# A macaron layer with float32 products from two float32r parts: filling PSUM banks in turns

## The chip, the cores and the metric

The kernel runs on one core of one Trainium2 chip. The metric is the device time of one launch in microseconds (us); every array is laid out by the host beforehand. The profile names the engines of the core as PE (TensorE matmul), PEld (its weight load), DVE (VectorE), ACT (ScalarE), POOL (GpSimd) and SP (SyncE, which issues DMAs here).

## The reference

The input x has the shape (4, 1024, 256) in float32. Three residual steps follow each other:

```python
x = x + 0.5 * ffn(layernorm(x), w1, w2, h1, h2, w3, scales)
x = x + attn(layernorm(x), log_dt, log_A_real, A_imag, C, W, b)
x = x + 0.5 * ffn(layernorm(x), w1, w2, h1, h2, w3, scales)

def tlin(x, w, s): return einsum('bsi,oi->bso', x, w) * s     # w holds only -1, 0 and 1
def ffn(x):                                                   # 256 -> 1024 -> 1024 -> 1024 -> 256
    h = silu(tlin(x, w1, w1_s)) * tlin(x, w2, w2_s)
    h = gelu(tlin(h, h1, h1_s))
    h = gelu(tlin(h, h2, h2_s))
    return tlin(h, w3, w3_s)
def attn(x):                                                  # S4D: a long convolution for each channel
    K = 2 * einsum('dn,dnl->dl', C', exp(dtA * t)).real       # taps of 1024 positions, 32 modes
    y = irfft(rfft(x_t, 2048) * rfft(K, 2048))[:, :, :1024]
    return gelu(y) @ W.T + b
```

## The kernel before

**Blocks and layers.** Each FFN works on 8 blocks of 512 tokens, named f0 to f7 in the first FFN and g0 to g7 in the second. f0 to f7, g0 and g1 go one by one through `ffn`; the last six go in three pairs through `ffn_pair`, whose wide layers are done with fewer products of half-size matrices. A wide input `t` is kept as two float32r parts: the high part is a cast on ACT (line 401), the low part is what the cast left, formed on DVE (`low_part`, line 309). Each linear layer then is two products for each 128 channels of input, one for each part, all summed in one PSUM bank (`linear`, lines 362 to 372, with the matmul at line 366). A bank of 128x512 float32 takes 4 products in the first layer (`pa` and `pb`, from `xt`), and 16 in the second and third (`p2`, `p3`, from `ha` and `h2`). The output layer takes 16 products for each of two banks (`po`, from `h3`, line 617 in `last_squares`). Behind each bank ACT applies silu or gelu (lines 384 and 399), and the next layer reads the result.

**Side work.** All else goes in between as a second stream. `kernel_steps` forms the S4D taps: sines and exponentials on ACT, products on DVE (`a_b`, `k_b`, `qd`, `p`), small matmuls into `pk` (line 883). `kernel_spectrum` takes their spectrum (`pf`). `mix` does the convolution of one batch and the multiplication by W (`pi`, line 1134, and `pw`, line 1159). The generator yields after a few operations, or yields PAUSE where it would wait. `tick` (line 1245) is called after each bank of a wide layer and lets side work run up to a count of work (STEP_WORK), or up to a PAUSE. `prepare` (line 1189), advanced by `ahead`, loads, normalises (`x_f`), moves and splits (`xt`) the next block. `weight_checks` (line 678) compares the weights with their signs on the fly, and sums the misses by one matmul (`p_bad`, line 724); if there were misses, a second copy of the layers would run.

**Order.** A scheduler reorders instructions within each engine when the program is built, by priorities and its own durations; then every engine runs its list in order and waits on semaphores. PSUM has 8 banks, all in one pool (tag "ps"). The names in the profile leave out the buffer numbers: `p_f` is p2 or p3 of some f block, `h_f` is h2 or h3.

Of the kernel before, what the change touches and what calls it, by code (L numbers as in the profile page):

```python
# [18 lines left out]
P = 128  # L19
B, L, D = 4, 1024, 256  # L20
HID = 1024
J = L // P
# [86 lines left out]
def macaron_layers(  # L109
# [24 lines left out]
    nc = tc.nc  # L134
# [224 lines left out]
            xt.append(t)  # L359
        return xt  # L360

    def linear(ps, w, m, acts):
        n = len(acts)
        for k in range(n):
            for part in range(parts):
                nc.tensor.matmul(  # L366
                    ps,
                    w[:, k, m * P : (m + 1) * P],
                    acts[k][:, part, :],
                    start=(k == 0 and part == 0),  # L370
                    stop=(k == n - 1 and part == parts - 1),
                )

    def ffn(xt, src, dst, blk, name, tick, ahead, final):


        ha = []
        for m in range(KH):
            pa, pb = bank(f"pa_{name}_{m}"), bank(f"pb_{name}_{m}")
            linear(pa, w1_sb, m, xt)  # L380
            linear(pb, w2_sb, m, xt)
            g = half(f"g_{name}_{m}")
            t = ring(f"ha_{name}_{m}", parts, TB, dtype=wide)
            nc.scalar.activation(g, pa, AF.Silu, scale=sc_sb[:, 0, m : m + 1])  # L384
            nc.vector.scalar_tensor_tensor(  # L385
                g if split else t[:, 0, :], pb, sc_sb[:, 1, m : m + 1], g, ALU.mult, ALU.mult
            )
            if split:
                nc.scalar.copy(t[:, 0, :], g)
                low_part(t, g)  # L390
            ha.append(t)
        for layer, w in ((2, h1_sb), (3, h2_sb)):
            hb = []
            for m in range(KH):
                ps = bank(f"p{layer}_{name}_{m}")
                linear(ps, w, m, ha)
                t = ring(f"h{layer}_{name}_{m}", parts, TB, dtype=wide)
                g = half(f"g{layer}_{name}_{m}") if split else t[:, 0, :]
                nc.scalar.activation(g, ps, AF.Gelu, scale=sc_sb[:, layer, m : m + 1])  # L399
                if split:  # L400
                    nc.scalar.copy(t[:, 0, :], g)  # L401
                    low_part(t, g)
                hb.append(t)
                ahead()
                if layer == 2 or m < KH - 1:
                    tick()
            ha = hb
        ahead(last=True)
        if name == "f0":
            nc.scalar.mul(w3s_half, w3s_half, 0.5)  # L410
        if final:
            last_tokens(ha, src, dst, blk, name)
        else:
            last_squares(ha, src, dst, blk, name)()

    def ffn_pair(xts, src, dst, blks, names, tick, ahead, final):

        pair_name = names[0]
        raw = raw_tiles(f"g_{pair_name}")
        for n, (xt, name) in enumerate(zip(xts, names)):  # L420
            for m in range(KH):
                pa, pb = bank(f"pa_{name}_{m}"), bank(f"pb_{name}_{m}")
                linear(pa, w1_sb, m, xt)
                linear(pb, w2_sb, m, xt)
                g = raw[m // QK, n][m % QK]
                nc.scalar.activation(g, pa, AF.Silu, scale=sc_sb[:, 0, m : m + 1])
                nc.vector.scalar_tensor_tensor(
                    g, pb, sc_sb[:, 1, m : m + 1], g, ALU.mult, ALU.mult
                )
            if n == 0:  # L430
                b11 = operand(raw[0, 0], f"b112_{pair_name}")
        calls = 0

        def step():
            nonlocal calls
            calls += 1
            if calls % 2 == 0:
                ahead()
                if calls < 2 * 7 * QK:
                    tick()  # L440

        raw, b11, _ = winograd(raw, b11, 2, pair_name, step)
        raw, c22, c12 = winograd(raw, b11, 3, pair_name, step)
        c11 = operand(raw[0, 0], f"hl00_{pair_name}")
        end_1 = last_squares(c12 + c22, src, dst, blks[1], names[1], QK)
        c21 = operand(raw[1, 0], f"hl10_{pair_name}")
        ahead(last=True)
        if final:
            end_1(nc.vector, nc.sync)
            last_tokens(c11 + c21, src, dst, blks[0], names[0])  # L450
        else:
            end_0 = last_squares(c11 + c21, src, dst, blks[0], names[0])
            end_1()
            end_0()
# [148 lines left out]
    def last_squares(acts, src, dst, blk, name, first=0):  # L603


        rest = []
        for k in range(DC):
            xr = half(f"xr_{name}_{k}", TB // SQ, SQ)
            for c in range(P // SQ):
                nc.sync.dma_start(xr[c * SQ : (c + 1) * SQ], in_squares(src, blk, k, c))  # L610
            rest.append(xr)
        banks = [bank(f"po_{name}_{k}") for k in range(DC)]
        order = [(first + k) % KH for k in range(KH)]
        for o, ps in enumerate(banks):
            for k in order:
                for part in range(parts):
                    nc.tensor.matmul(  # L617
                        ps,
                        w3_sb[:, k, o * P : (o + 1) * P],
                        acts[k][:, part, :],  # L620
                        start=(k == order[0] and part == 0),
                        stop=(k == order[-1] and part == parts - 1),
                    )

        def end(add_on=nc.gpsimd, queue=stores):
            for k, ps in enumerate(banks):
                o, y = half(f"o_{name}_{k}"), half(f"y_{name}_{k}", TB // SQ, SQ)
                nc.scalar.activation(o, ps, AF.Identity, scale=w3s_half[:, k : k + 1])
                nc.vector.transpose(y, o.rearrange("p (n s) -> p n s", s=SQ))  # L629
                add_on.tensor_tensor(y, rest[k], y, ALU.add)  # L630
                for c in range(P // SQ):
                    queue.dma_start(in_squares(dst, blk, k, c), y[c * SQ : (c + 1) * SQ])

        return end
# [198 lines left out]
    def kernel_steps():  # L833
# [7 lines left out]
        for g0 in range(0, DD, group):  # L841
# [58 lines left out]
            for d1 in range(0, group, n):  # L900
                re, im = fine

                def outer(coarse, t):
                    return (
                        coarse[:, d1 : d1 + n, :, None].to_broadcast(shape),
                        t[:, d1 : d1 + n, None, :].to_broadcast(shape),
                    )

                a, o = (half(f"{t}_{g0 + d1}", n, A1, A0) for t in ("p", "po"))
                tt(a, *outer(to_re, re), ALU.mult)  # L910
                tt(o, *outer(to_im, im), ALU.mult)
                tt(a, a, o, ALU.add)
                ready.append((d1, a))
                if len(ready) == 4:
                    for old in ready[0:2]:
                        products(*old)
                    del ready[0:2]
                yield
            yield PAUSE
            for old in ready:  # L920
# [115 lines left out]
    def mix(b, xn):  # L1036
# [109 lines left out]
        for j in range(0, J, 2):  # L1146
            xr = half(f"xr_{b}_{j}", 2, D)
            nc.sync.dma_start(xr, positions(x1, b, j))
            todo.append((j, xr))
            if len(todo) == 1:  # L1150
                continue
            yield PAUSE
            results = []
            for j, xr in todo:
                ps = bank(f"pw_{b}_{j}")
                results.append(ps)
                for e in range(2):
                    for dc in range(DC):
                        nc.tensor.matmul(  # L1159
                            ps[:, e * D : (e + 1) * D],  # L1160
                            yts[dc][j // JQ][:, (j % JQ + e) * P : (j % JQ + e + 1) * P],
                            wt_sb[:, dc, :],
                            start=(dc == 0),
                            stop=(dc == DC - 1),
                        )
            yield PAUSE
            for (j, xr), ps in zip(todo, results):
                y = half(f"yw_{b}_{j}", 2, D)
                tt(
                    y,  # L1170
                    ps.rearrange("p (e d) -> p e d", e=2),
                    bias_sb[:, None, :].to_broadcast([P, 2, D]),
                    ALU.add,
                )
                nc.gpsimd.tensor_tensor(y, xr, y, ALU.add)
                stores.dma_start(positions(x2, b, j), y)
            todo = []
# [208 lines left out]
```

## Time and profile before

| | us |
|---|---|
| median of 3 runs | 1369.99 |
| lowest and highest run | 1369.08, 1370.74 |
| the profiled execution | 1368.44 |
| its span | 1366.6 |
| PE busy in it | 1351.7 |
| DVE busy | 1010.7 |
| ACT busy | 776.5 |
| POOL busy | 287.9 |

The profile shows one execution. A row of its timeline has the start in us from the span's start, the busy time, the engine, the line, the operation, what it writes and reads, and how many instructions are merged into the row; in square brackets stands the idle time before the row and which engine's work ended it. The durations of rows overlap within an engine, since the next instruction starts before the last one's end is recorded: for what an instruction costs its engine, the distance between starts is used. PEclk is the granted clock of TensorE, in this execution 0.998 of full speed in the mean.

### The profile page before, as it was taken

Reading aid. Unit: us, or ns where it says so; the run is one execution under the profiler, and the core shown is the slowest. Engines: PE = TensorE matmul, PEld = TensorE weight load, DVE = VectorE, ACT = ScalarE, POOL = GpSimd, SP = SyncE. Lnnn points to the kernel's source line nnn. Section 1 sums busy time; section 2 is a strip of 40 time slices with the busy share of each in tenths; the row PEclk is TensorE's granted clock in tenths of the full one; section 3 lists DMA queues with packets and bytes.
Section 4 is the critical chain, followed back from the end, with each engine's and each line's share of the span. In section 5 each row is a group of like instructions: output and inputs, shape, how many; then the busy total and the mean of one; then the engine's idle time right before and its main releaser. Section 6 shows DMA issues by size and latency. Waiting matters only on the chain.

```text
span 1366.6 us, 18200 instructions
## 1 busy us (share of the span) xinstructions
PE 1351.7 (99%) x6300; PEld 1124.7 (82%) x6300; DVE 1010.7 (74%) x1889; ACT 776.5 (57%) x1236; POOL 287.9 (21%) x443
## 2 busy tenths in 40 slices
PE   8999999999999999999999999999999999999997
PEld 7888878888888888888888887888888888888886
DVE  6997885749965887668855799658885778568654
ACT  5985966454444543534545745436776576656663
POOL 4440220421205213420114012052300430040000
PEclk9999999999999999999999999999999999999999
DMA  9440121413125235354054352352655145521441
GB/s 357 109 142 5 31 62 39 143 36 123 40 93 199 64 108 190 122 183 123 23 168 116 112 154 47 116 168 79 212 160 168 31 141 179 173 64 62 162 131 49
DMA packets 125637, 159.99 MB, mean 117 GB/s; under 512 B 77968, under 2 KB 88208, under 8 KB 120160
## 3 DMA queue, kind: packets, MB, share of 16 engines
q1 hardware_dynamic: 103520, 99.94, 24.2%
q0 software_dynamic: 21744, 58.55, 13.6%
q8 instruction: 51, 0.84, 0.2%
q14 instruction: 50, 0.41, 0.1%
q10 hardware_dynamic: 272, 0.26, 0.1%
HBM read 120.95 MB, written 37.75 MB: 116 GB/s over the span
## 4 chain that ended last, share of the span: by engine, by line
PE 49%; DVE 4%; DMA 0%; issue 0%; ACT 0%; SPq 0%; DVEq 0%
PE p_g L366 7%; PE p2a_g L510 6%; PE p3a_g L510 6%; PE p3x_g L510 5%; PE p2x_g L510 5%; PE p_f L366 4%; PE pa_g L366 4%; PE pb_g L366 4%; PE po_g L617 3%; PE pi L1134 1%; PE pw L1159 1%; DVE y L155 1%; PE po_f L617 1%; PE pa_f L366 1%; PE pb_f L366 1%; PE pf_m L956 1%
## 5 line engine op out<-in xcount | busy, mean ns | idle before, releaser
L366 PE MATMUL p_f<-ha_f,h_sb 128*128 128x512 f32 x1024 | 238.7, 392 | 0.1
L366 PE MATMUL p_f<-h_f,h_sb 128*128 128x512 f32 x1024 | 237.1, 391 | 0.0
L366 PEld LDWEIGHTS p_f<-h_f,h_sb 128*128 128x128 f32 x1024 | 192.1, 188 | 39.7
L366 PEld LDWEIGHTS p_f<-ha_f,h_sb 128*128 128x128 f32 x1024 | 191.4, 188 | 40.4 <-DVE ha_f L309 0.8
L399 ACT ACTIVATE g_f<-p_f,sc_sb 128x512 f32<-128x512 f32 x128 | 87.4, 689 | 210.6 <-PE p_f L366 183.0
L309 DVE TENSOR_TENSOR h_f<-g_f,h_f 128x512 fp32r<-128x512 f32 x128 | 87.9, 689 | 112.8 <-ACT h_f L401 112.5
L401 ACT CAST h_f<-g_f 128x512 fp32r<-128x512 f32 x128 | 78.4, 619 | 3.1
L524 ACT ACTIVATE h_g<-h_g,sc_sb 128x512 f32<-128x512 f32 x72 | 52.0, 723 | 43.8 <-DVE h_g L480 43.6
L339 POOL DMA_DIRECT2D moved<-sq_f x56 | 30.6, 554 | 198.3 <-DVE sq_f L155 198.3
L366 PE MATMUL pa_f<-xt_f,w_sb 128*128 128x512 f32 x256 | 70.5, 391 | 1.3 <-DVE xt_f L321 0.7
L339 POOL DMA_DIRECT2D moved<-sq_g x64 | 34.9, 552 | 167.1 <-DVE sq_g L155 165.9
L366 PE MATMUL pb_f<-xt_f,w_sb 128*128 128x512 f32 x256 | 69.9, 389 | 0.0
L366 PE MATMUL pa_g<-xt_g,w_sb 128*128 128x512 f32 x256 | 68.9, 389 | 0.0
L366 PE MATMUL pb_g<-xt_g,w_sb 128*128 128x512 f32 x256 | 68.9, 389 | 0.0
L617 PE MATMUL po_f<-h_f,w_sb 128*128 128x512 f32 x256 | 60.7, 391 | 1.6 <-ACT h_f L401 0.9
L385 DVE SCALAR_TENSOR_TENSOR g_f<-pb_f,sc_sb,g_f 128x512 f32<-128x512 f32 x64 | 46.6, 745 | 20.2 <-ACT g_f L384 10.5
L366 PE MATMUL p_g<-ha_g,h_sb 128*128 128x512 f32 x256 | 59.4, 391 | 0.1
L366 PE MATMUL p_g<-h_g,h_sb 128*128 128x512 f32 x256 | 59.3, 391 | 0.0
L630 POOL TENSOR_TENSOR y_g<-xr_g,y_g 128x512 f32<-128x512 f32 x12 | 17.0, 1424 | 197.5 <-DVE y_g L629 183.8
L617 PEld LDWEIGHTS po_f<-h_f,w_sb 128*128 128x128 f32 x256 | 47.6, 188 | 13.0 <-DVE h_f L309 2.0
L366 PEld LDWEIGHTS pa_f<-xt_f,w_sb 128*128 128x128 f32 x256 | 48.0, 188 | 12.2 <-DVE xt_f L356 1.0
L399 ACT ACTIVATE g_g<-p_g,sc_sb 128x512 f32<-128x512 f32 x32 | 22.1, 689 | 60.8 <-PE p_g L366 49.5
(302 smaller groups left out, 2879.9 us busy)
## 6 DMA issues: line engine op xcount, KB each, us to landing
w<-q SPq DMA_DIRECT2D x42, 1024.0 KB, 5.0
q<-s POOLq DMA_DIRECT2D x40, 256.0 KB, 4.3
h_sb<-in_h_dram POOLq DMA_DIRECT2D x8, 1024.0 KB, 14.2
given<-in_h_dram SPq DMA_DIRECT2D x32, 256.0 KB, 3.4
kr<-k_hat SPq DMA_DIRECT2D x20, 256.0 KB, 2.7
ki<-k_hat SPq DMA_DIRECT2D x20, 256.0 KB, 3.0
q<-h_sb POOLq DMA_DIRECT2D x16, 256.0 KB, 4.4
xr_f<-in_x_dram SPq DMA_DIRECT2D x64, 64.0 KB, 2.5
```

Source lines behind the costliest of these rows:

```text
L155: return op(dst, *args, **kwargs)
L309: return nc.vector.tensor_tensor(t[:, 1, :], src, t[:, 0, :].bitcast(F32), ALU.subtract)
L339: stores.dma_start(moved[k].rearrange("(c r) a q -> a r c q", r=SQ)[a], sq[a * SQ : (a + 1) * SQ].rearrange("r c j s -> r c (j s)"),)
L366: nc.tensor.matmul(ps, w[:, k, m * P : (m + 1) * P], acts[k][:, part, :], start=(k == 0 and part == 0), stop=(k == n - 1 and part == parts ...
L385: nc.vector.scalar_tensor_tensor(g if split else t[:, 0, :], pb, sc_sb[:, 1, m : m + 1], g, ALU.mult, ALU.mult)
L399: nc.scalar.activation(g, ps, AF.Gelu, scale=sc_sb[:, layer, m : m + 1])
L401: nc.scalar.copy(t[:, 0, :], g)
L510: nc.tensor.matmul(ps, weights[:, c, m * P : (m + 1) * P], ops[c][:, part, :], start=(first and c == 0 and part == 0), stop=(c == QK - 1 a ...
L524: nc.scalar.activation(o, src, AF.Gelu, scale=sc_sb[:, layer, m : m + 1])
L617: nc.tensor.matmul(ps, w3_sb[:, k, o * P : (o + 1) * P], acts[k][:, part, :], start=(k == order[0] and part == 0), stop=(k == order[-1] an ...
L630: add_on.tensor_tensor(y, rest[k], y, ALU.add)
L956: nc.tensor.matmul(ps[e][:, part, :], m[:, e, part, :], rows_of(q + JQ * e), start=True, stop=True)
```

## The change

`linear` now takes a list of banks with their weights and fills them in turns: for each input of 128 channels all the banks' products of both parts. `pa` and `pb` of the first layer are filled in turns in `ffn` and `ffn_pair`, and so are the first two banks of each wide layer of `ffn`, both ahead of the activations and of the ticks of either. In the output layer the loop over inputs goes outside the loop over the two banks. The taps' products are issued in groups of four steps rather than two, and the four banks of `pw` in one group rather than two, so that a mix yields PAUSE twice less. No matmul is added or taken away.

```diff
--- before.py
+++ after.py
@@ -359,17 +359,20 @@
             xt.append(t)
         return xt
 
-    def linear(ps, w, m, acts):
+    def linear(outs, acts):
+
+
         n = len(acts)
         for k in range(n):
-            for part in range(parts):
-                nc.tensor.matmul(
-                    ps,
-                    w[:, k, m * P : (m + 1) * P],
-                    acts[k][:, part, :],
-                    start=(k == 0 and part == 0),
-                    stop=(k == n - 1 and part == parts - 1),
-                )
+            for ps, w, m in outs:
+                for part in range(parts):
+                    nc.tensor.matmul(
+                        ps,
+                        w[:, k, m * P : (m + 1) * P],
+                        acts[k][:, part, :],
+                        start=(k == 0 and part == 0),
+                        stop=(k == n - 1 and part == parts - 1),
+                    )
 
     def ffn(xt, src, dst, blk, name, tick, ahead, final):
 
@@ -377,8 +380,7 @@
         ha = []
         for m in range(KH):
             pa, pb = bank(f"pa_{name}_{m}"), bank(f"pb_{name}_{m}")
-            linear(pa, w1_sb, m, xt)
-            linear(pb, w2_sb, m, xt)
+            linear([(pa, w1_sb, m), (pb, w2_sb, m)], xt)
             g = half(f"g_{name}_{m}")
             t = ring(f"ha_{name}_{m}", parts, TB, dtype=wide)
             nc.scalar.activation(g, pa, AF.Silu, scale=sc_sb[:, 0, m : m + 1])
@@ -391,9 +393,14 @@
             ha.append(t)
         for layer, w in ((2, h1_sb), (3, h2_sb)):
             hb = []
+            first = [bank(f"p{layer}_{name}_{m}") for m in range(2)]
+            linear([(ps, w, m) for m, ps in enumerate(first)], ha)
             for m in range(KH):
-                ps = bank(f"p{layer}_{name}_{m}")
-                linear(ps, w, m, ha)
+                if m < 2:
+                    ps = first[m]
+                else:
+                    ps = bank(f"p{layer}_{name}_{m}")
+                    linear([(ps, w, m)], ha)
                 t = ring(f"h{layer}_{name}_{m}", parts, TB, dtype=wide)
                 g = half(f"g{layer}_{name}_{m}") if split else t[:, 0, :]
                 nc.scalar.activation(g, ps, AF.Gelu, scale=sc_sb[:, layer, m : m + 1])
@@ -420,8 +427,7 @@
         for n, (xt, name) in enumerate(zip(xts, names)):
             for m in range(KH):
                 pa, pb = bank(f"pa_{name}_{m}"), bank(f"pb_{name}_{m}")
-                linear(pa, w1_sb, m, xt)
-                linear(pb, w2_sb, m, xt)
+                linear([(pa, w1_sb, m), (pb, w2_sb, m)], xt)
                 g = raw[m // QK, n][m % QK]
                 nc.scalar.activation(g, pa, AF.Silu, scale=sc_sb[:, 0, m : m + 1])
                 nc.vector.scalar_tensor_tensor(
@@ -610,9 +616,10 @@
                 nc.sync.dma_start(xr[c * SQ : (c + 1) * SQ], in_squares(src, blk, k, c))
             rest.append(xr)
         banks = [bank(f"po_{name}_{k}") for k in range(DC)]
+
         order = [(first + k) % KH for k in range(KH)]
-        for o, ps in enumerate(banks):
-            for k in order:
+        for k in order:
+            for o, ps in enumerate(banks):
                 for part in range(parts):
                     nc.tensor.matmul(
                         ps,
@@ -911,10 +918,10 @@
                 tt(o, *outer(to_im, im), ALU.mult)
                 tt(a, a, o, ALU.add)
                 ready.append((d1, a))
-                if len(ready) == 4:
-                    for old in ready[0:2]:
+                if len(ready) == 6:
+                    for old in ready[0:4]:
                         products(*old)
-                    del ready[0:2]
+                    del ready[0:4]
                 yield
             yield PAUSE
             for old in ready:
@@ -1147,7 +1154,7 @@
             xr = half(f"xr_{b}_{j}", 2, D)
             nc.sync.dma_start(xr, positions(x1, b, j))
             todo.append((j, xr))
-            if len(todo) == 1:
+            if len(todo) < J // 2:
                 continue
             yield PAUSE
             results = []
```

## The prediction

> **What bounds the kernel now.** I read the page first: busy shares, then the chain that ended last. Then the waits of the tensor engine (PE), then windows and timelines at each layer boundary.
>
> ```profile
> PE 1351.7 (99%) x6300; PEld 1124.7 (82%) x6300; DVE 1010.7 (74%) x1889; ACT 776.5 (57%) x1236; POOL 287.9 (21%) x443
> PE 49%; DVE 4%; DMA 0%; issue 0%; ACT 0%; SPq 0%; DVEq 0%
> ```
>
> PE is busy for 99% of the span. The change removes and adds no matmul, so it can only win what PE loses. From start to start a 128x512 float32r product takes 226.7 ns, and I summed such pitches over all PE records: 1342.0 us of 1355.6 us from first to last. So about 13.7 us are lost, 3.7 of them in the warm-up products at the start and 1.7 in scattered switches of 0.02 us. The rest is 2.6 at the groups of taps, 0.9 where the second layer waits for the first, 4.9 where the output layers wait (f0 0.33, f1 2.16, f4 0.06, f6 0.87, g0 1.47), and 0.3 at p_bad. Of the 4.9 the waits view shows 2.5 as such (its columns: us in total, times, longest); the rest is in late starts between two such waits:
>
> ```profile
> PE po_f L617 <- ACT h_f L401: 0.9, 1, 0.9
> PE po_f L617 <- DVE h_f L309: 0.7, 1, 0.7
> PE po_g L617 <- DVE h_g L309: 0.6, 1, 0.6
> PE po_g L617 <- ACT h_g L401: 0.3, 1, 0.3
> ```
>
> So the whole prize is below 9 us (0.6%). What can be lost is larger: where another engine carries no slack, any work put ahead of an activation stops PE. The windows show such a place. The columns are stretch, length, then busy us of PE, PEld, DVE, ACT, POOL, and PEclk:
>
> ```profile
> 53.10:82.20 29.10, 29.10 (x130) 24.08 (x130) 28.56 (x62) 27.61 (x35) 16.77 (x31) 1.00 0.53 186
> 82.20:90.00 7.80, 7.80 (x34) 5.98 (x33) 7.80 (x15) 7.49 (x11) 0.00 (x0) 1.00 0.42 66
> ```
>
> That is the third layer of the first block (f0) and its output layer. VectorE (DVE) has 0.5 us to spare in 29 and none in the next 8. The timeline of the boundary shows who is just in time:
>
> ```profile
> 82.15 6.21 PE L617 MATMUL po_f<-h_f,w_sb 128*128 128x512 f32 x25
> 84.56 0.60 ACT L401 CAST h_f<-g_f 128x512 fp32r<-128x512 f32 x1
> 86.61 0.68 DVE L309 TENSOR_TENSOR h_f<-g_f,h_f 128x512 fp32r<-128x512 f32 x1
> ```
>
> The last high part is cast at 84.56, and the low part of h3_f0_7, the last one, starts at 86.61. The output layer still ran into only 0.33 us of idle time there. The chain of reason: f0's DVE queue sets when its output layer may end.
>
> **The change, part by part.**
>
> *Filling banks in turns, by itself.* 227 ns a product, also where the bank changes:
>
> ```profile
> 22.31 1.07 PE L366 MATMUL pa_f<-xt_f,w_sb 128*128 128x512 f32 x4
> 23.22 1.07 PE L366 MATMUL pb_f<-xt_f,w_sb 128*128 128x512 f32 x4
> ```
>
> Four products and a change of bank take 23.22 - 22.31 = 0.91 us, that is 4 x 0.2267. The Trainium skill speaks against the change here: "TensorE: Matmul & The Clock Gate", section "A second HAM failure mode: psum-queue depth-cycling", tells of a kernel that cycled its banks and lost throughput as the clock fell and rose between bursts. With the row: 0. With the rule, half clock for part of the run, tens of us. The row decides: bank changes are common before, and PEclk stays at 1.00. I take 0.
>
> *pa and pb in turns, and the start of the second layer.* pa ends 0.9 us later than before (four products), with pb, so the last silu starts later by as much. Against that, with two banks filled in turns the second layer reaches its last input after 28 products instead of 14, 3.2 us more cover. The two waits there, at 107.0 (0.49) and 845.3 (0.37), go: **-0.86**.
>
> *Output layer, both banks in turns.* In the source order the last input is needed after 14 products, then after 28: cover 28 x 0.2267 = 6.35 us instead of 3.17. But the build's scheduler moves instructions within each engine. In the order of PE before, it already mixes the two banks wherever it held h3_7 for late: the high and low part are first used as product 19 and 22 in f0, 28 in f1, 29 and 30 in f6, 28 to 30 in g0. So only f2 to f5, f7 and g1 get more cover, and these lose nothing in the trace (f4: 0.06). Gain: about 0; those of f1 (2.16), f6 (0.87) and g0 (1.47) aren't reached by it.
>
> *Taps in groups of four steps.* The loop's rows:
>
> ```profile
> 218.34 2.05 PE L883 MATMUL pk<-qd,p 128*64 128x32 f32 x32
> 220.32 3.92 PE L366 MATMUL p_f<-ha_f,h_sb 128*128 128x512 f32 x16
> 224.18 1.99 PE L883 MATMUL pk<-qd,p 128*64 128x32 f32 x31
> ```
>
> One cycle is 5.84 us: 16 x 0.2267 = 3.63, 32 x 0.0584 = 1.87, and 0.34 for the two edges of a group. Eight groups become six in the new order (a group of three steps, one of one, one of four, in each half): **-0.7**. The `pw` groups of four banks save two switches of 0.02 a batch: below 0.1, nothing. The late taps are copied by ScalarE (0.215 us each) earlier or later in the same layer; nobody waits for them before the next layer.
>
> *First two banks of the wide layers in turns.* Here it goes wrong. Bank 0 of h2 ends after 30 products instead of 16: 24.12 + 30 x 0.2267 = 30.9. Then come gelu, gelu and cast (0.69, 0.69, 0.60 in this trace): the low part of h2_f0_0 starts at about 33.0, where it started at
>
> ```profile
> 29.89 0.69 DVE L309 TENSOR_TENSOR h_f<-g_f,h_f 128x512 fp32r<-128x512 f32 x1
> ```
>
> Normally DVE would catch up, but both banks' matmuls also stand before the side work of two ticks, and the new order puts more of it ahead of the activations. Between the low part of h2_f0_0 and that of h3_f0_7, DVE has 152 instructions instead of 134. The added ones stand behind h3_f0_7 in before:
>
> ```profile
> 88.48 0.68 DVE L155 TENSOR_TENSOR a_b<-a_b,e_b 128x512 f32<-128x512 f32 x1
> 89.09 0.68 DVE L155 TENSOR_TENSOR k_b<-k_b,e_b 128x512 f32<-128x512 f32 x1
> 91.50 1.71 DVE L155 TENSOR_TENSOR qd<-k_b,a_b 64x256 f32<-64x256 f32 x4
> 94.53 1.94 DVE L155 TENSOR_SCALAR x_f<-x_f,mv_f,rstd_f 128x256 f32<-128x256 f32 x4
> ```
>
> Four a_b/k_b at 0.60 (start to start) 2.4, four qd 1.7, a cast and two reciprocals 0.6, less one short k_b that goes ahead 0.4, and eight x_f: 0.46 each in the row above (three starts in 1.94 - 0.56), 0.32 where one stands alone (825.80 to 826.12), so 2.6 to 3.7. Together 6.9 to 8.0; I take +7.2. Before, the way from low part to low part took 86.61 - 29.89 = 56.7. So the last one starts at 33.0 + 56.7 + 7.2 = 96.9 and ends by 97.6; without any idle time of DVE (2.5 us in before's 56.7) at 95.1. PE needs it as product 36 (eight products of the next block stand between): 82.25 + 36 x 0.2267 = 90.4. The stall is 4.7 to 7.2. ScalarE bounds it too: g3_f0_7 now stands behind two table loads (1.28 each) and two Sin (0.63, 0.71) that read a_b, so its cast ends at 93.4 to 94.5 against a need at 88.6: 4.8 to 5.9. Both together about 7.0 instead of 0.33: **+6.7**.
>
> A rule of the same page (the table under "What's actually happening") is that after an idle window of about 3.4 us the clock halves and needs as long busy to return. The longest wait of PE after the start in before is 0.9 us and PEclk is 1.00, so the trace doesn't test it. It would add at most 3.4 / 2 = 1.7. But PE's idle time here comes in pieces (low part 5, high part 7, low part 7), none surely as long: I take 0 and keep 1.7 for the range.
>
> *The same at other blocks,* by the same sums of queued DVE rows against PE's need. f1: order as before, ScalarE a little later: **+0.3**. f6: two groups of `pf` (3.45 us each) move from the third layer into the second, so DVE has less PE time to hide in; the last low part comes 9.9 after the last p3 instead of 7.1, the need is 6.9: 2.9 instead of 0.87, **+2.0**. g0: casts and a normalise stand ahead of h3_7; 10.75 against a need of 7.5: 3.2 instead of 1.47, **+1.8**. p_bad now stands directly behind p3_g1_4, while the reduction to total stands some four DVE operations behind the low part of h3_g1_3. Before, PE had 16 `pw` products between and just met it:
>
> ```profile
> 898.73 0.69 DVE L309 TENSOR_TENSOR h_g<-g_g,h_g 128x512 fp32r<-128x512 f32 x1 [1.37 <-ACT h_g L401]
> 900.70 0.19 PE L724 MATMUL p_bad<-ones,total 128*1 128x1 f32 x2
> ```
>
> Now total comes 4.3 us after p3_g1_3's end and PE arrives 3.6 after it (16 products): 1.1 with the handing over (0.44 from 900.26 to 900.70), instead of 0.27, **+0.85**. f2 to f5, f7, g1 and the three pairs: no wait (f3 is within 0.2 us of one). Three more table loads on ScalarE, hidden under 43% idle time. DMA queues: the loads of `xr` for the second half of a mix are issued one tick earlier on SP, its stores two; they land in 2.5 us and DMA is half idle, so 0.
>
> **Sum.** 6.7 + 2.0 + 1.8 + 0.85 + 0.3 - 0.86 - 0.7 = +10.1, on the profiled execution's 1368.4: 1378.5. The median of the runs is 1.6 above that execution: 1380.
>
> **Rivals.**
> (a) The faster side: the low parts reach PE in time, as DVE does the moved work in its idle time, and the doubled cover works as the source says. Then -0.86 and -0.7, and of the 4.9 at the output layers about 3.5: 1365. For it: DVE is idle for a quarter of the span. Against: not in f0, where 0.5 us of 29 is free. It decides at one point, the start of the low part of h3_f0_7: before 90 this holds, at 91 f0 still costs nothing more than before, each us beyond is one lost.
> (b) Little happens: the built order before had the turns already, so nothing is won; f0 loses 2 to 3, f6 and g0 nothing: 1370 to 1373. For it: my sums of queued work take DVE to idle as in before, and ScalarE alone would give the lower end of f0's stall.
> (c) The clock falls in f0's gap and f6 and g0 lose more by the queue behind it: 1382 to 1386.
>
> **How the numbers follow.** My forecast (1373 to 1384) has 0.68, (c) 0.12, (b) 0.13, (a) 0.07. Leaving out (a) and the ends, the range is 1371.5 to 1386. What a measurement can tell from no change is 0.2%, 2.7 us: faster than 1367.3 has 0.06, within has 0.10 ((b)'s greater part), slower 0.84.
>
> **What would show it.** In the profile after: the largest PE wait is po_f on h_f at 86 to 97 us, 5 us or more in sum; po_f and po_g waits grow at f6 and g0; the rows `pk` stand in six groups. I am wrong if DVE's low part of h3_f0_7 starts before 91, or if p_f on ha_f at 107 us still waits.

## The result, and the profile after

The changed kernel takes 1381.77 us (median of 4 runs, 1380.31 to 1385.6) against 1369.53 before (4 runs): the ratio is 1.0096, with a 95% interval of 1.0076 to 1.0116. It is slower by about 12 us. The forecast was 1380, slower by 10.

The page of the profiled execution (1380.31 us, span 1378.5) begins:

```profile
PE 1354.8 (98%) x6300; PEld 1126.3 (82%) x6300; DVE 1008.2 (73%) x1889; ACT 776.4 (56%) x1240; POOL 287.7 (21%) x443
```

No engine does noticeably more work. What grew is the idle time of PE, and the view of its waits names the places (columns as before: us in total, times, longest):

```profile
PE po_f L624 <- ACT h_f L408: 4.4, 3, 2.5
PE pa_f L369 <- DVE xt_f L356: 3.2, 1, 3.2
PE po_f L624 <- DVE h_f L309: 2.2, 3, 0.8
PE pa_g L369 <- DVE xt_g L356: 1.9, 1, 1.9
PE po_g L624 <- DVE h_g L309: 0.7, 1, 0.7
PE p_bad L731 <- ACT g_g L406: 0.7, 1, 0.7
```

The table has the whole of it, summed as in the prediction: the distance between the starts of two PE instructions, less the pitch of the first (226.7 ns for a 128x512 float32r product), in us. A stretch in which TensorE was granted half its clock ("half clock" below) shows as loss too. At f6 and g0 part of the loss is a wait of the next block's first products (`pa`), which the built order has among those of the output layer.

| place | before | after |
|---|---|---|
| start (to 10.6 us) | 4.03 | 3.62 |
| f0, output layer | 0.32 | 5.79 |
| f1 and g1, second layer | 0.86 | 0 |
| groups of taps | 2.52 | 1.89 |
| f1, output layer | 2.16 | 4.47 |
| f6, output layer | 0.87 | 5.09 |
| g0, output layer | 1.47 | 3.86 |
| p_bad | 0.27 | 1.06 |
| two short waits in wide layers (154, 521 us) | 0 | 0.69 |
| rest, scattered | 1.16 | 0.79 |
| all | 13.66 | 27.26 |

From PE's first instruction to its last it is 13.6 us longer, the span 12.0. The 1.6 between them lie behind the last matmul: the end came 8.3 us after its start before, 6.7 now, and in the experiments between 6.7 and 8.2. No run was made on that.

At f0 the rows that answer to those of before are these, from the timeline:

```profile
32.48 0.69 DVE L309 TENSOR_TENSOR h_f<-g_f,h_f 128x512 fp32r<-128x512 f32 x1 [2.40 <-ACT h_f L408]
...
81.71 4.69 PE L624 MATMUL po_f<-h_f,w_sb 128*128 128x512 f32 x20
...
89.73 1.28 ACT L406 ACT_TABLE_LOAD   x1
91.02 0.69 ACT L406 ACTIVATE g_f<-p_f,sc_sb 128x512 f32<-128x512 f32 x1
92.41 0.73 PE L624 MATMUL po_f<-h_f,w_sb 128*128 128x512 f32 x2 [2.55 <-ACT h_f L408]
94.69 0.69 DVE L309 TENSOR_TENSOR h_f<-g_f,h_f 128x512 fp32r<-128x512 f32 x1
95.44 0.74 PE L624 MATMUL po_f<-h_f,w_sb 128*128 128x512 f32 x2 [0.69 <-DVE h_f L309]
```

The first low part of the second layer starts at 32.48 instead of 29.89, the last of the third at 94.69 instead of 86.61. The last gelu (91.02) stands behind a table load, and that behind two Sin. About 4.3 us of f0's loss are waits for high parts from ScalarE. The last low part alone would have held PE for 5.5 of the 5.79: it ends at 95.38, and as product 36 it was needed at 81.71 + 36 x 0.2267 = 89.87. In the windows view the same stretch shows PE idle for 4.3 of 14.6 us and DVE for 0.1, at full clock:

```profile
53.10:81.70 28.60, 28.60 (x127) 23.66 (x127) 27.58 (x64) 28.28 (x38) 15.18 (x27) 1.00 0.47 158
81.70:96.30 14.60, 10.29 (x40) 6.82 (x39) 14.52 (x31) 10.85 (x14) 0.00 (x0) 1.00 0.23 36
```

From the first of these low parts to the last, DVE (third figure) had 2.3 us of idle time before and 2.7 now, and 5.1 us more work. The same view has before's stretch first, then the changed kernel's:

```profile
29.89:86.61 56.72, 56.72 (x251) 46.51 (x250) 54.38 (x135) 50.82 (x68) 22.60 (x41) 1.00 0.58 162
32.48:94.69 62.21, 58.59 (x254) 46.99 (x253) 59.50 (x152) 55.34 (x72) 22.49 (x40) 1.00 0.53 139
```

At f1 there is something that the profiled execution of before does not have. The waits are 1.60 and 0.72, and then products take 0.43 us each from start to start, up to 190.1:

```profile
184.25 0.73 PE L624 MATMUL po_f<-h_f,w_sb 128*128 128x512 f32 x2 [1.60 <-ACT h_f L408]
185.70 0.73 PE L624 MATMUL po_f<-h_f,w_sb 128*128 128x512 f32 x2 [0.72 <-DVE h_f L309]
...
187.32 0.63 PE L369 MATMUL pb_f<-xt_f,w_sb 128*128 128x512 f32 x1
187.75 0.63 PE L369 MATMUL pa_f<-xt_f,w_sb 128*128 128x512 f32 x1
```

The windows view gives a granted clock of 0.57 there (eighth figure, 186 to 190 us):

```profile
186.00:190.00 4.00, 4.00 (x12) 3.09 (x11) 2.74 (x5) 2.97 (x4) 1.47 (x2) 0.57 0.56 88
```

Eight products at 0.2 us more are 1.6 us. At f6 the same happens behind a gap of 3.35 us, with about 1.4 us. What PE waits for there is the cast of the next block's input, which stands on DVE just ahead of the last low part:

```profile
653.68 0.75 DVE L356 CAST xt_f<-xf_f 128x512 fp32r<-128x512 f32 x2
654.15 0.79 PE L369 MATMUL pa_f<-xt_f,w_sb 128*128 128x512 f32 x1 [3.19 <-DVE xt_f L356]
654.35 0.68 DVE L309 TENSOR_TENSOR h_f<-g_f,h_f 128x512 fp32r<-128x512 f32 x1
```

### The profile page after: what moved, and what is told of

Read it like the earlier page. It is cut to its first block, busy times and chain, and to the rows that moved or that the text cites. A ratio compares the mean times of both kernels' runs of the same rounds, so it can differ in the third digit from the quotient of the medians.

```text
span 1378.5 us, 18204 instructions
## 1 busy us (share of the span) xinstructions
PE 1354.8 (98%) x6300; PEld 1126.3 (82%) x6300; DVE 1008.2 (73%) x1889; ACT 776.4 (56%) x1240; POOL 287.7 (21%) x443
## 3 DMA queue, kind: packets, MB, share of 16 engines
q0 software_dynamic: 21744, 58.55, 13.7%
## 4 chain that ended last, share of the span: by engine, by line
PE 83%; DVE 10%; ACT 3%; DMA 3%; issue 1%; POOL 0%; DVEq 0%; POOLq 0%; ACTq 0%
PE p_f L369 24%; PE p_g L369 6%; PE p3a_g L516 6%; PE p2a_g L516 6%; PE p3x_g L516 5%; PE p2x_g L516 5%; PE pa_g L369 4%; PE pb_g L369 4%; PE pa_f L369 4%; PE pb_f L369 4%; PE po_g L624 3%; PE po_f L624 3%; PE pi L1141 2%; PE pw L1166 2%; PE pf_m L963 2%; DVE y L155 2%
## 5 line engine op out<-in xcount | busy, mean ns | idle before, releaser
L369 PE MATMUL pa_f<-xt_f,w_sb 128*128 128x512 f32 x256 | 82.6, 398 | 3.9 <-DVE xt_f L356 3.2
L369 PE MATMUL pb_f<-xt_f,w_sb 128*128 128x512 f32 x256 | 81.6, 394 | 0.0
L369 PE MATMUL pa_g<-xt_g,w_sb 128*128 128x512 f32 x256 | 79.2, 389 | 1.9 <-DVE xt_g L356 1.9
L369 PE MATMUL pb_g<-xt_g,w_sb 128*128 128x512 f32 x256 | 79.0, 389 | 0.0
```

What stands on the lines that cost most here:

```text
L369: nc.tensor.matmul(ps, w[:, k, m * P : (m + 1) * P], acts[k][:, part, :], start=(k == 0 and part == 0), stop=(k == n - 1 and part == parts ...
```

## The experiments

The theory was that turns in the wide layers delay the first activation, that the scheduler answers by another order on DVE and ScalarE, and that the stalls at f0, f6 and g0 are those queues. The rivals were that cycling banks costs PE itself, that the late activation costs by itself, and that the mix, the taps or the output layer are to blame. The losses at the places that matter, of the profiled executions (half clock included, marked *):

| run | f0 | f1 | f6 | g0 | p_bad | ratio to before, 95% interval |
|---|---|---|---|---|---|---|
| before | 0.32 | 2.16 | 0.87 | 1.47 | 0.27 | |
| changed | 5.79 | 4.47* | 5.09* | 3.86 | 1.06 | 1.0096 (1.0076 to 1.0116) |
| second layer alone | 6.08* | 2.10 | 1.83 | 1.47 | 0.27 | 1.0059 (1.0042 to 1.0076) |
| third layer alone | 0.32 | 2.19 | 1.72 | 5.39* | 0.27 | 1.0035 (1.0022 to 1.0047) |
| mix alone | 0.34 | 2.15 | 3.88* | 1.47 | 1.05 | 1.0033 (1.0021 to 1.0046) |
| taps alone | 0.33 | 2.58 | 1.34 | 1.46 | 0.27 | 1.0000 (0.9991 to 1.0009) |
| half turns | 0 | 2.08 | 0.88 | 1.47 | 0.27 | 1.0004 (0.9996 to 1.0013) |
| without wide | 0 | 2.61 | 2.29 | 1.49 | 1.04 | 1.0015 (1.0009 to 1.0022) |
| narrow turns | 0 | 3.76* | 1.21 | 1.49 | 0.27 | 0.9996 (0.9988 to 1.0004) |
| best | 0 | 4.22* | 0 | 0 | 0.27 | 0.9966 (0.9952 to 0.9980) |
| issue order | 0.33 | 2.17 | 1.43 | 1.46 | 0.27 | one execution |
| changed, again | 6.08* | 2.86 | 4.93* | 5.42* | 1.05 | one execution |
| mix alone, again | 0.32 | 3.73* | 2.29 | 1.47 | 1.05 | one execution |

**The second layer alone.** Turns for the first two banks of h1 only:

```diff
         for layer, w in ((2, h1_sb), (3, h2_sb)):
+            turns = layer == 2
+            first = [bank(f"p{layer}_{name}_{m}") for m in range(2 if turns else 0)]
+            if turns:
+                linear([(ps, w, m) for m, ps in enumerate(first)], ha)
...
```

> Only the first two banks of the second layer (h1) are filled in turns; all else as before. Theory (late first activation): bank 0 ends 3.2 us later, its activation and low part start later, and the scheduler puts work ahead of h3_f0_7; so f0's output layer stalls by 5.5 to 7 us near 86 to 97 us, the waits of the second layer for the first (0.87) go, the taps stand in more and smaller groups (+0.6 to 0.9): 1374 to 1377. f6 and g0 as before. Rival (filling in turns costs PE by itself): a loss at each of the ten blocks' second layers, or products slower than 227 ns, and no large wait at f0. Rival (the third layer's turns or po's order are the cause): 1369 or less.

Measured: 1376.39 us, f0 lost 6.08. The whole of f0's loss comes from this part, at one place: the other nine blocks have the same turns, and none loses over 1 us more than before at its output layer. That rules out the turning of banks as a cost of PE. The waits at f0 are those of the changed kernel within 0.03 us (0.48, 0.96 and 2.72 here). One of the nine isn't as before, against the expectation: f6 lost 0.96 more. The taps stand in 13 groups instead of 8, as expected in kind. In the waits of PE:

```profile
PE po_f L625 <- ACT h_f L409: 3.7, 3, 2.6
PE po_f L625 <- DVE h_f L309: 1.5, 2, 0.8
PE p_f L367 <- DVE h_f L309: 1.1, 1, 1.1
```

The third line is a wait in a wide layer near 518 us, which the expectation had not.

**The third layer alone.** The same edit with `turns = layer == 3`.

> Only the first two banks of the third layer (h2) are filled in turns. Theory: f0 is as before (0.3 us lost there), g0's last low part is late by 2 to 3 us more, nothing else moves: 1371 to 1373. Rival (third layer's turns are what delays h3_f0_7): f0 loses 5 or more, 1375 or above. Rival (the cover of 28 products helps): 1369 or less.

Measured: 1373.09 us. f0 is as before, and g0 lost 5.39, of which about 1.6 is half clock. f6 lost 0.85 more, which was not expected. What PE waits for at g0 is the next block's cast, which stands on DVE just ahead of the last low part:

```profile
829.83 0.75 DVE L356 CAST xt_g<-xf_g 128x512 fp32r<-128x512 f32 x2
830.30 0.80 PE L367 MATMUL pa_g<-xt_g,w_sb 128*128 128x512 f32 x1 [1.90 <-DVE xt_g L356]
830.50 0.68 DVE L309 TENSOR_TENSOR h_g<-g_g,h_g 128x512 fp32r<-128x512 f32 x1
```

**The mix alone.**

```diff
-            if len(todo) == 1:
+            if len(todo) < J // 2:
                 continue
```

> Only the pw products of a mix go in one group of four banks, two PAUSEs fewer. Theory: the mixes run ahead by ticks, f6 gets more side work ahead of its last low part and loses 2 to 4 us more[...], p_bad 0.8: 1372 to 1374. Rival (pw grouping saves switches and does nothing else): 1369.5, no wait at f6 beyond 0.9.

Measured: 1373.22 us. p_bad loses as in the changed kernel. f6 loses only half as much more as there: its gap is 1.78, not 3.35, and without the half clock it loses 2.3 (1.4 more than before), not 3.7. f5 lost 0.96, which was not expected. The larger group of `pw` doesn't pay for that. The rival, that it only saves switches, falls.

**The taps alone.**

```diff
-                if len(ready) == 4:
-                    for old in ready[0:2]:
+                if len(ready) == 6:
+                    for old in ready[0:4]:
                         products(*old)
-                    del ready[0:2]
+                    del ready[0:4]
```

> Only the taps' products go in groups of four steps. Theory: four groups instead of eight, each with edges of 0.32 us: -1.3, nothing else moves: 1368.3. Rival (larger groups make DVE or ScalarE late, as the taps' copies come in a bunch): 1370 or more, with a new wait of PE behind the pk rows.

Measured: no difference (1369.02 us against 1368.4, ratio 1.0000). The groups halved as expected, 64 products together and so four pairs of edges instead of eight:

```profile
111.80 4.24 PE L367 MATMUL p_f<-ha_f,h_sb 128*128 128x512 f32 x18
115.97 3.92 PE L884 MATMUL pk<-qd,p 128*64 128x32 f32 x64
119.82 2.56 PE L367 MATMUL p_f<-ha_f,h_sb 128*128 128x512 f32 x10
```

That is 1.26 us less. It came back nearly whole: f1 lost 0.42 more, f6 0.47 more, and a wait near 145 us some 0.2. At f6 PE arrives 0.48 earlier and goes on at the same time as before. At f1 it arrives 0.24 earlier and goes on 0.18 later.

**Half turns.** The second layer takes only four of eight inputs in turns, then finishes bank 0 and bank 1:

```diff
+        order = [(k, out) for k in range(min(n, turns)) for out in outs]
+        order += [(k, out) for out in outs for k in range(turns, n)]
+        for k, (ps, w, m) in order:
...
```

> As the run with the second layer alone, but only the first four of eight inputs are taken in turns, then each bank is finished: bank 0 ends after 24 products (1.8 us later than before, not 3.2), the last input is needed as product 22. In its order DVE has 132 instructions ahead of h3_f0_7, as before (133), not 151. Queue theory: f0 loses 0.3 as before, the 0.87 between the first and second layer goes, f6 as before or 1 more; 1368 to 1370. Rival (the late first activation by itself delays DVE's queue): f0 loses 2 to 3.5, 1371 to 1373.

Measured: 1369.75 us, ratio 1.0004. The activation of bank 0 is late by more than half as much as with full turns (24 products instead of 30, against 16), but DVE has 132 instructions between the same two low parts, and not 151, and the output layer of f0 runs through:

```profile
83.53 7.42 PE L627 MATMUL po_f<-h_f,w_sb 128*128 128x512 f32 x32
...
89.24 0.69 DVE L309 TENSOR_TENSOR h_f<-g_f,h_f 128x512 fp32r<-128x512 f32 x1
```

So f0 pays for the reordered queues at least for the most part: the last low part starts 5.7 us after the output layer's first product here, 4.5 in before (86.61 - 82.15) and 13.0 in the changed kernel (94.69 - 81.71). The delay of full turns with the order of before was not run. By an estimate from this trace it would not be free: here the last low part ends at 89.93 and is needed as product 30, at 83.53 + 30 x 0.2267 = 90.33, so of the other 6 products' delay (1.4 us) about 1.0 would be lost. Another 0.64 is lost here at 99.6 us, in the next block's first layer.

**The issue order.** Both banks issued ahead of the ticks, but filled one after the other.

```diff
+            first = [bank(f"p{layer}_{name}_{m}") for m in range(2)]
+            for m, ps in enumerate(first):
+                linear([(ps, w, m)], ha)
...
```

> Both banks of each wide layer are issued ahead of their activations and ticks, but filled one after the other as before. Theory of the forecast's sentence on ticks: the side work of two ticks behind the second bank delays DVE, part of f0's loss. Rival: the scheduler orders by readiness, so the issue order counts for nothing: f0 as before (0.3), 1368 to 1370.

Measured: 1368.65 us in one execution, f0 0.33, and the order of f0's instructions on DVE is that of before. Where the source puts the two linears counts for nothing there. It isn't without effect everywhere: from 608.9 us on the lists differ, a group of `pf` stands later in f6's third layer, and f6 lost 1.43 instead of 0.87. That the scheduler goes by readiness is argued, not shown.

**Without the wide layers' turns,** all other parts of the change kept.

> The changed kernel without turns in the wide layers. Theory: f0 back to 0.3, g0 to 1.5, f1 to 2 to 2.6; f6 keeps its loss of 3 to 4 and p_bad 1, since they come from the mix; second layer's wait for the first 0.9 back: 1371 to 1374. Rival (the parts only hurt together, or the output layer's order hurts): 1377 or more.

Measured: 1370.59 us, just under the range given. f0 and g0 are back, p_bad keeps 1.04, f6 keeps 2.29: less than with the mix alone since no half clock followed. So of some 12 us, the wide layers bring about 10.

**Narrow turns.** Only pa/pb and the output layer in turns.

> Only pa/pb of the first layer and the two banks of the output layer are filled in turns; wide layers, taps and mix as before. Theory: nothing in it pays: the scheduler had the output layer's banks in turns where h3_7 came late (f1, f6, g0), so their 2.2, 0.9 and 1.5 stay; f0's 0.33 and f4's 0.06 go; 0.4 of the second layer's wait may change by 0.2: 1368 to 1368.6 on a base of 1368.4. Rival (double cover works): f1, f6 and g0 lose 3 us less: 1365. Rival (cycling banks costs clock): slower, above 1370.

Measured: 1368.07 us against 1368.0. The cover of 28 products took away f0's 0.33 and f4's 0.06, but PE then lost 0.30 at 91 us, where the next block's low part comes late. It gave nothing at f1, f6 and g0, where the built order had the banks in turns already. What f1 lost more is half clock, behind the same gaps as before. Filling banks in turns costs nothing either.

**A better version.** Without the mix's larger group, with turns of the second layer in f1 and g1 only, and with a tick left out. Everything else is as in the changed kernel; the cut shows the two places against the run with the second layer alone:

```diff
-            turns = layer == 2
+            turns = layer == 2 and name in ("f1", "g1")
...
-                if layer == 2 or m < KH - 1:
+                if layer == 2 or m < KH - {"f6": 2, "g0": 2}.get(name, 1):
                     tick()
```

> Before, with pa/pb, po and taps as in the change, turns of the second layer in f1 and g1 only, the mix as before, and no tick ahead of the last bank of the third layer in f6 and g0. Theory: -0.9 between the layers, -0.6 to -1.3 taps, f6 and g0 lose none of 0.87 and 1.47, f0 none of 0.33; f1 keeps 2.2 to 2.6: 1364 to 1365.5. Rival (the side work that is pushed back stalls a later layer by as much): 1368 or more.

Measured: 1365.01 us, ratio 0.9966 (0.9952 to 0.9980); it beats both kernels. What each of its parts brings was not run apart. In its waits only f1's output layer is left of those above:

```profile
PE po_f L623 <- ACT h_f L408: 1.3, 1, 1.3
PE po_f L623 <- DVE h_f L309: 0.7, 1, 0.7
```

**One step further,** ticks left out at f1, f3 and f5, so that f1's gelu has no Sin ahead of it.

> As the run before it (best), but the ticks left out stand elsewhere: two ahead of the last banks of the third layer in f1 and in f5, one in f3, none in f6 and g0. Theory: ScalarE has no Sin ahead of g3_f1_7, so f1 loses 0 instead of 2.6 and the fall of the clock behind it (1.6); g0 gets about 1 back: 1361.5 to 1363.5. Rival (the Sin and table loads that are pushed back delay f2's layers by as much): 1365 or more.

Measured: 1365.3 us, ratio 0.9977 (0.9968 to 0.9987), no better than the last. f1 lost nothing, but the load of g2's input came late. In the profiled execution (1368.68 us, the slowest of ten) that cost 4.49 at 918 to 925 us, half clock included:

```profile
921.04 0.43 DVE L356 CAST xt_g<-xf_g 128x512 fp32r<-128x512 f32 x1 [5.52 <-DMA xf_g<-moved]
921.53 0.79 PE L367 MATMUL pa_g<-xt_g,w_sb 128*128 128x512 f32 x1 [2.65 <-DVE xt_g L356]
```

The last mix was not late: its last addition starts at 910.24, against 910.81 in the better version. But g2's last two loads, issued from 912.40 on, took 8.6 and 9.4 us to land, where all four took 2.9 to 3.3 in the better version; the DMA engines were 99% busy from 915 to 920 us (88% there). One of the two was also issued 2.7 us later than there. That the side work pushed back brought this about is not shown. So the rival was right in its time and in that the wait moved, but the wait is not in f2's layers.

**The half clock, again.** Two programs were run once more to see whether it belongs to the program.

> The changed kernel once more, written with the same source in another order of lines. If the falls of the clock at f1 and f6 follow from the order alone, both are there again; [...]one or both may be absent, or one be seen at f0 or g0, while all waits of PE stay within 0.3 us. 1378 to 1384.

> The run with the mix alone once more: its f6 had 1.8 us of idle time and then a half clock; without the wide layers' turns the same idle time had none. If chance decides, the half clock may be absent here, with the same idle times: f6 loses 2.3 or 3.9.

Measured: 1381.12 and 1372.77 us. The changed kernel's idle times are the same within 0.05 us (2.73 and 2.72 at f0, 1.76 and 1.77 at f1, 3.35 and 3.35 at f6, 2.07 and 2.07 at g0), yet the half clock now came at f0, f6 and g0 and not at f1, where the loss was 2.86 instead of 4.47. At f0 it added only 0.3 (6.08 against 5.79): the slow products fill time in which PE had waited for the last low part. The mix's f6 had its 1.78 again and no half clock behind it; f1 had one this time, behind gaps that the first run passed at full clock. The windows view of the first mix run, then of the second, 651 to 654 us (products in brackets, granted clock eighth figure):

```profile
651.00:654.00 3.00, 3.00 (x8) 2.37 (x8) 2.46 (x5) 2.97 (x4) 1.04 (x1) 0.52 0.00 0
```

```profile
651.00:654.00 3.00, 3.00 (x14) 2.44 (x13) 2.16 (x6) 2.97 (x5) 1.29 (x1) 1.00 0.00 0
```

## Why the prediction was right, and where it was not

- **f0: right in place and kind, a little too large.** Forecast +6.7, measured +5.5, within the stall of 4.7 to 7.2 from which the upper end was taken. The first low part started at 32.48 (forecast 33.0, with PE 0.44 us earlier in this execution), the last at 94.69. The mis-sized term is the work added to DVE from low part to low part, taken at +7.2. DVE's busy time grew by 5.1. The added rows are those that were named, and cost 6.8 net; rows that stand in both took 1.6 less, and no run was made on why. DVE's idle time did not shrink: 2.7 us, where before had 2.3. So it is luck that the end (95.38) lies at 95.1, the sum without idle time. The high part was bound by ScalarE as said, at 92.36 rather than 93.4 to 94.5.
- **The reason given beside it was wrong.** The prediction said that both banks' matmuls stand ahead of two ticks' side work, and put part of the shift down to it. The issue order alone changed nothing at f0, and with half turns both banks stand ahead of the ticks too, without a loss there. The queues carry most of the loss, as forecast; that the scheduler chose them because bank 0 ends later in its own reckoning is argued, not shown.
- **f6, g0, p_bad: right in kind, f6 and g0 somewhat small.** Forecast +2.0, +1.8 and +0.85; measured +4.2 (2.8 without the half clock), +2.4 and +0.8. At f6 the last low part came 9.7 after the last p3, where 9.9 was said. What the prediction left together the runs parted: g0 is the third layer's turns, p_bad the mix. At f6 the parts share it: alone the mix brings 1.4 without the half clock, the second layer's turns 0.96, the third's 0.85.
- **f1: the term that failed most.** Forecast +0.3, measured +2.3. ScalarE came later by 0.7 against PE, and the half clock was the other 1.6. The half clock isn't bound to the change: the repeated execution of the changed kernel had none, and narrow turns had one behind the gaps of before.
- **Second layer's wait -0.86, taps -0.7: right** (-0.86, and -0.63 in six groups), though the taps alone show that such a gain is no gain in time as long as a late activation stands behind it.
- **The clock was weighed and taken at 0: wrong.** The case against was that no gap would hold a window of 3.4 us. In this execution it fell behind f1's gaps of 1.77 and 0.89 us, and at f6 behind 3.35; each fall cost 1.4 to 1.6 us. Rival (c) had it in the range, at 1382 to 1386, but at f0, where it came in the repeated execution (1381.12 us).
- **Rival (a)** put its point at a low part before 90; it came at 94.69. **Rival (b)** fell too: f0 lost 5.79, and f6 and g0 lost more than before.
- Two things weren't forecast: 0.7 us of short waits inside wide layers, and the end 1.6 us nearer to the last matmul.
- **The sum is closer than its terms.** In the profiled execution it came to +11.9 against +10.1. f0 was 1.2 too large, and the end took back 1.6; the half clock's 3.0, f6, g0, f1 and the short waits were too small or absent. So the queues were forecast by reasoning, but the total near 1380 is in part luck. In the list of what PE loses before, the terms add up to 14.1, not 13.7: the scattered part is about 1.2.

## What to carry to other kernels

Where an engine is at 99%, price a new order of its work by what that does to the queues behind it: compare the built orders of the other engines ahead of the last producers, and sum what now stands in front. More cover at one place is worth only what the next late producer doesn't take back, so find all places that wait, and remove work ahead of the last activation before you regroup matmuls. Then test each part alone: here two parts were free, one was given back, and three cost time, each mostly at places of its own.

## What the runs showed of the hardware that was not expected

The granted clock fell to half behind idle times far below the 3.4 us that the prediction took from the page: 2.2 us idle within 3.4 (1.78 in one piece) in the mix's first run, about 2.6 in the better version's f1. With the same idle times it didn't fall in other executions (2.2 in the mix's second run, 2.6 without the wide layers; even 2.9 at f0 in the first execution of the changed kernel). The clearest pair is f1 in before and in narrow turns, with gaps of 1.05 and 0.89 in both. The windows view of before, then of narrow turns, shows the same busy time of PE and another clock behind it:

```profile
177.80:181.20 3.40, 1.79 (x7) 0.84 (x7) 3.33 (x9) 1.32 (x3) 0.00 (x0) 1.00 0.41 65
181.80:184.80 3.00, 3.00 (x14) 2.45 (x14) 1.80 (x3) 2.39 (x3) 1.40 (x2) 1.00 0.45 71
```

```profile
177.80:181.20 3.40, 1.79 (x7) 0.87 (x6) 3.33 (x9) 1.31 (x3) 0.00 (x0) 1.00 0.43 69
181.80:184.80 3.00, 3.00 (x9) 2.31 (x8) 1.89 (x4) 2.25 (x4) 1.32 (x2) 0.50 0.46 72
```

"TensorE: Matmul & The Clock Gate" of the Trainium skill says under "Why this matters for your kernels" to allow no gaps above some 3 us; the runs say that a gap of 1 to 2 us with others close behind is already a draw of about 1.5 us. How the chance depends on the gap isn't settled: there are too few cases. The swings of the clock of which the page's "A second HAM failure mode: psum-queue depth-cycling" tells didn't come with the turns here: products took 227 ns in turns and one by one, and narrow turns measured 0.9996.
